# Square roots of layer norms and key lengths as exponential of a logarithm, in a graph transformer kernel

## The chip, the core and the metric

The kernel runs on one core of one Trainium2 chip. A core has five engines that run their own instruction queues in order and wait for each other through semaphores: TensorE (PE in the profile; its weight loads are PEld), VectorE (DVE), ScalarE (ACT), GpSimd (POOL) and SyncE (SP), which only issues DMAs here. The metric is device time in microseconds (us) of one execution.

## The reference

A graph of 3125 nodes with 256 features and 100000 edges passes through two layers, each a graph branch and a mixing branch on the same normalised input, then a feed-forward part.

```python
xn = _layernorm(x, axis=-1)                      # (x - m) / sqrt(v + eps)
x = x + _L0_gnn_ref(xn, ...) + _L0_mix_ref(xn[None], ...)[0]
x = x + _L0_ffn_ref(_layernorm(x, axis=-1)[None], ...)[0]
xn = _layernorm(x, axis=-1)
x = x + _L1_gnn_ref(xn, edge_index, edge_attr_64, ...) + _L1_mix_ref(xn[None], ...)[0]
x = x + _L1_ffn_ref(_layernorm(x, axis=-1)[None], ...)[0]
```

What matters here is where a square root or an exponential is taken:

- `_L0_gnn_ref`: two graph convolutions with 4 heads. Each takes a softmax over the edges of a node (exponentials), and is followed by a batch norm over all nodes, `(x - mean) * rsqrt(var + EPS)`.
- `_L0_mix_ref`: four layers of linear attention. Each has two layer norms, a softmax of the queries and of the keys (exponentials), and a feed-forward part with an exact GELU.
- `_L0_ffn_ref`: 16 experts, of which each token takes two. The two gate values go through a softmax. ReLU inside, a layer norm at the end.
- `_L1_gnn_ref`: one graph convolution with 8 heads and edge features, with the softmax over edges.
- `_L1_mix_ref`: queries and keys are divided by their lengths, `t / maximum(norm(t), 1e-12)`, and enter a second-order expansion.
- `_L1_ffn_ref`: half of the tokens, by the rank of a learned weight, pass through an MLP with the tanh form of GELU.

## The kernel before

**Tiles.** The 3125 nodes are 25 tiles of 125 (`P`), handled in 7 groups of up to four (`k.groups`, six of 4 tiles and one of 1). A layer norm of a group is: `bn_stats` and `bn_aggr` on VectorE for mean and variance (`mv`), a square root with `EPS` added on ScalarE, a reciprocal on VectorE (`rs`, 125 x 4 values), and the scaling of the tiles by it. `ln_stats` (from line 137) does it once for all 25 tiles at the start; `group_stats` (from line 2139) does it for a group in the expert stage and in the last stage.

**Layer 0** runs both branches at once. `SlotOrder.run` writes out by hand the order of the convolution on TensorE, VectorE and ScalarE (`manual_schedule`): for each of 63 steps GpSimd gathers key and value rows (line 707), VectorE multiplies and sums them with the query (lines 1074 and 1077) and takes the maximum (lines 1087 to 1091), ScalarE takes the Exp (line 1101), VectorE sums it (line 1108) and weights the values (line 1114), TensorE adds them up (line 200), and ScalarE copies the sum out (`accT`, line 1133). Four buffers hold the gathered rows. At the marks `m` in that order the planner `Filling` puts pieces of the mixing branch in between. A `Piece` has a weight `w`, a TensorE part `pe`, a part `post` for the other engines, and the pieces that it depends on; the planner issues as much weight at each `m` as its share of the whole comes to, takes the first piece of a window of 8 whose dependencies are done, and issues a piece's `post` only after the TensorE part of the next one. The norm of a group is four pieces (`norm_pieces`, from line 1649): `stats` with the square root (line 1661), `scaled` with the reciprocal (line 1666), the negative mean (line 1667) and the scaling on ScalarE (line 1672), and two that turn the result (lines 1682 and 1689). Line 1763 and line 1821 are the Exps of this branch, line 1999 its GELU.

After each of the two convolutions the batch norm's scale is formed in place (lines 1586 to 1592: aggregate, square root, reciprocal, products).

**The expert stage** (`l0_ffn_routed`) leaves the order to the scheduler. Routing: a norm per group, gate values, the two best of 16 (`top2`, with an Exp at line 2115), and scatters of the tokens to the experts' slots. Then 16 experts, two matrix products each. Then the return, group by group: GpSimd gathers the two results of each token (line 707, tile `g`), VectorE adds them (line 2338), one norm ends the expert layer (lines 2345 and 2348), a second one begins layer 1 (line 152), TensorE turns it and forms the keys and values, which VectorE adds and SP stores (line 2362).

**Layer 1's convolution** (`EdgeOrder`) is again an order by hand, with edge features turned, copied and multiplied (lines 1289, 1295, 1305), added on VectorE (line 1316), and the softmax Exp at line 1324. Pieces of the second mixing branch (`l1_mix_pieces`) fill it. Its planner, `Mixing`, is a little different: a piece has a third part `act`, issued together with `pe`, its `post` comes at the beginning of the next `m`, and a piece with no `post` counts as done at once. Some pieces were already put into the return from the experts (`begin.mixing.ahead`). The branch runs over two halves of the heads, in each over 7 groups of keys and then 7 groups of queries. A group has a head and a body; `spread` puts the pieces of the next group's head behind given places of this group's body, and what has no place behind its end. A head loads the features (`p0`), projects them (`p1`, ending with a Square on ScalarE), and takes the lengths (`p2`): TensorE sums the squares by head (line 3043), ScalarE takes the square root (line 3052, 125 x 16 values), VectorE takes a maximum with 1e-12 and a reciprocal (lines 3095 and 3096 for keys, 3247 and 3248 for queries). For keys the rows follow (line 3114) and `finished` scales them (line 3129); the Squares of the body use the lengths as their scale (line 3168). For queries the lengths are spread over the features by a copy, a transpose and another copy (`widened`, `spread4`, `brought`).

**The last stage** (`l1_ffn`): for each group a norm, a transpose, the row of weights; the row goes to memory and back, VectorE ranks all tokens (line 3606), and the MLP with its GELU (line 3566) runs beside it. The scheduler orders it.

ScalarE evaluates a function from a table that holds a set of functions. The program has an explicit load (`ACT_TABLE_LOAD` in the profile) wherever the next function is not in the set that is loaded; a load stands under the line of the function that it is for. No load stands ahead of a copy, an Identity, a Square or a ReLU in this program.

Of the kernel before, what the change touches and what calls it, by code (L numbers as in the profile page):

```python
# [10 lines left out]
F32 = mybir.dt.float32  # L11
# [8 lines left out]
P = 125  # L20
# [113 lines left out]
    return ap.rearrange("(i p) d -> p i d", p=P)  # L134


def ln_stats(k, pool, src):

    nc = k.nc
    st = pool.tile([P, k.NT, 6], F32, name="ln_st", tag="ln_st")  # L140
    mv = pool.tile([P, k.NT, 2], F32, name="ln_mv", tag="ln_mv")
    rs = pool.tile([P, k.NT], F32, name="ln_rs", tag="ln_rs")
    for i in range(k.NT):
        nc.vector.bn_stats(st[:, i], src[:, i])
        nc.vector.bn_aggr(mv[:, i], st[:, i])
    nc.scalar.activation(rs, mv[:, :, 1], AF.Sqrt, bias=k.eps[:P], scale=1.0)
    nc.vector.reciprocal(rs, rs)
    return mv, rs


# [1303 lines left out]
def l0_gnn_slots(k, dram, order, a, y, pp, pq, cw, filling, tmp):  # L1454
# [45 lines left out]
    with k.tc.manual_schedule(engines=ORDERED):  # L1500
        mix.ahead(30.0)
        prev = None
        for n in (1, 2):
# [81 lines left out]
            prev = hsp  # L1585
            for c in range(2):
                nc.vector.bn_aggr(bmv[:, c], bst[:, c])
            nc.scalar.activation(sc, bmv[:, :, 1], AF.Sqrt, bias=k.eps, scale=1.0)
            nc.vector.reciprocal(sc, sc)
            nc.vector.tensor_tensor(sc, sc, gam, op=ALU.mult)  # L1590
            nc.vector.tensor_tensor(sh, bmv[:, :, 0], sc, op=ALU.mult)
            nc.vector.tensor_tensor(sh, bet, sh, op=ALU.subtract)
# [44 lines left out]
def l0_mix_pieces(k, dram, a, y, wts, one, wp, hp, hp2, pp):  # L1637
# [11 lines left out]
    def norm_pieces(g, deps, weights, free):  # L1649

        g0, ng = k.groups[g]
        o = {}

        def stats():
            st = wp.tile([P, 4, 6], F32, name="ln_st", tag="ln_st")
            o["mv"] = mv = wp.tile([P, 4, 2], F32, name="ln_mv", tag="ln_mv")
            o["rs"] = rs = wp.tile([P, 4], F32, name="ln_rs", tag="ln_rs")
            for j in range(ng):
                nc.vector.bn_stats(st[:, j], y[:, g0 + j])
                nc.vector.bn_aggr(mv[:, j], st[:, j])  # L1660
            nc.scalar.activation(rs[:, :ng], mv[:, :ng, 1], AF.Sqrt, bias=k.eps[:P], scale=1.0)

        def scaled():
            mv, rs = o["mv"], o["rs"]
            nm = wp.tile([P, 4], F32, name="ln_nm", tag="ln_nm")
            nc.vector.reciprocal(rs[:, :ng], rs[:, :ng])
            nc.vector.scalar_tensor_tensor(
                nm[:, :ng], mv[:, :ng, 0], -1.0, rs[:, :ng], op0=ALU.mult, op1=ALU.mult
            )
            o["xh"] = xh = wp.tile([P, 4, D], F32, name="xh", tag="xh")  # L1670
            for j in range(ng):
                nc.scalar.activation(  # L1672
                    xh[:, j], y[:, g0 + j], AF.Identity, bias=nm[:, j : j + 1],
                    scale=rs[:, j : j + 1],
                )

        def turn(c):
            if c == 0:
                o["hT"] = hp2.tile([128, 2, 4 * P], F32, name="hTm", tag="hTm")
            o[c] = ps = ps_tile()  # L1680
            for j in range(ng):
                nc.tensor.transpose(  # L1682
                    ps[:, j * P : j * P + P], o["xh"][:, j, c * 128 : c * 128 + 128],
                    k.ident[:P, :P],
                )

        def bring(c):
            gam, bet = weights()
            nc.scalar.activation(
                o["hT"][:, c, : ng * P], o[c][:, : ng * P], AF.Identity,  # L1690
                bias=bet[:, c : c + 1], scale=gam[:, c : c + 1],
            )

        p1 = Piece(small, None, stats, [*deps, *scales])
        p2 = Piece(small, None, scaled, [p1, *free])
        scales[:] = [p2]
        ts = [Piece(us(ng * P), lambda c=c: turn(c), lambda c=c: bring(c), [p2]) for c in range(2)]
        return [p1, p2, *ts], o
# [440 lines left out]
def group_stats(k, wp, src, ng):  # L2139

    nc = k.nc
    st = wp.tile([P, 4, 6], F32, name="ln_st", tag="ln_st")
    mv = wp.tile([P, 4, 2], F32, name="ln_mv", tag="ln_mv")
    rs = wp.tile([P, 4], F32, name="ln_rs", tag="ln_rs")
    for j in range(ng):
        nc.vector.bn_stats(st[:, j], src[:, j])  # L2146
        nc.vector.bn_aggr(mv[:, j], st[:, j])
    nc.scalar.activation(rs[:, :ng], mv[:, :ng, 1], AF.Sqrt, bias=k.eps[:P], scale=1.0)
    nc.vector.reciprocal(rs[:, :ng], rs[:, :ng])
    return mv, rs  # L2150


# [840 lines left out]
def l1_mix_pieces(k, tabs, a, pl):  # L2993
# [44 lines left out]
        nc.scalar.activation(sq[:, :w_], x[:, :w_], AF.Square)  # L3038

    def by_heads(o, src):  # L3040
        o["p"] = ps = ps_tile()
        for j in range(o["ng"]):
            nc.tensor.matmul(
                ps[:P, j * 4 : j * 4 + 4], src[:, j * P : j * P + P], head0, start=True, stop=True
            )
# [3 lines left out]
        return o[name][:, : o["ng"] * 4]  # L3049

    def root(o):
        nc.scalar.activation(row4(o, "r4"), o["p"][:P, : o["ng"] * 4], AF.Sqrt)

    def widened(o, name):
        n = o["ng"] * 4
# [31 lines left out]
    for c in range(2):  # L3087
        C = {}

        def key_head(g, o, deps, c=c):  # L3090
            ng = o["ng"]

            def lengths():
                r = o["r4"][:, : ng * 4]
                nc.vector.tensor_scalar(r, r, 1e-12, 1.0 / s, op0=ALU.max, op1=ALU.mult)
                nc.vector.reciprocal(r, r)

            def rows(j0, n):
                o["p"] = ps = ps_tile()
                for b in range(n):  # L3100
                    tk = slice((j0 + b) * P, (j0 + b + 1) * P)
                    at = ps[:P, b * D : b * D + D]
                    for ci in range(2):
                        nc.tensor.matmul(
                            at[:, 128:], o["xT"][:, ci, tk],
                            wqkv[:, ci, 2 * D + c * 128 : 2 * D + c * 128 + 128],
                            start=(ci == 0), stop=(ci == 1),
                        )
                    nc.tensor.transpose(at[:, :128], o["x"][:, tk], k.ident)

            def rows_out(j0, n):
                if j0 == 0:
                    o["kv"] = wp.tile([P, 4, 257], F32, name="kvt", tag="kvt")
                nc.scalar.copy(
                    o["kv"][:, j0 : j0 + n, :D],
                    o["p"][:P, : n * D].rearrange("p (b d) -> p b d", d=D),
                )

            def finished():
                kv = o["kv"][:, :ng]  # L3120
                nc.vector.memset(kv[:, :, D:], 1.0)
                v = kv[:, :, 128:D]
                nc.vector.tensor_tensor(
                    v, v, bv[:, c * 128 : c * 128 + 128].unsqueeze(1).to_broadcast([P, ng, 128]),
                    op=ALU.add,
                )
                for j in range(ng):
                    kk = kv[:, j, :128].rearrange("p (h d) -> p h d", d=32)
                    nc.vector.tensor_tensor(
                        kk, kk,  # L3130
                        o["r4"][:, j * 4 : j * 4 + 4].unsqueeze(2).to_broadcast([P, 4, 32]),
                        op=ALU.mult,
                    )

            p0 = Piece(0.0, act=fn(load, o, g, False), deps=deps)
            p1 = Piece(2.3, fn(project, o, 2 + c), deps=[p0], act=fn(squared, o, 2 + c, 1.0))
            p2 = Piece(0.9, lambda: by_heads(o, o["sq"]), lengths, [p1], fn(root, o))
            ps = [
                Piece(0.8 * min(2, ng - j0), fn(rows, j0, min(2, ng - j0)), None, [p1],
                      fn(rows_out, j0, min(2, ng - j0)))  # L3140
                for j0 in range(0, ng, 2)
            ]
            p3 = Piece(0.1, None, finished, [p2, *ps])
            return [p0, p1, p2, *ps, p3]

        def key_body(g, o, head, c=c, C=C):
            ng, g0 = o["ng"], o["g0"]
            p2, p3 = head[2], head[-1]

            def squares():  # L3150
                o["k2"] = wp.tile([P, 4, 128], F32, name="k2", tag="k2")
# [90 lines left out]
        def query_head(g, o, deps, c=c, C=C):  # L3242
            ng, w_ = o["ng"], o["w_"]

            def lengths():
                r = o["r4"][:, : ng * 4]
                nc.vector.tensor_scalar_max(r, r, 1e-12)
                nc.vector.reciprocal(r, r)

            def scaled():  # L3250
                x = o["x"][:, :w_]
                nc.vector.scalar_tensor_tensor(
# [27 lines left out]

            p0 = Piece(0.0, act=fn(load, o, g, True), deps=deps)
            p1 = Piece(2.3, fn(project, o, c), deps=[p0], act=fn(squared, o, c, s))
            p2 = Piece(0.9, lambda: by_heads(o, o["sq"]), lengths, [p1], fn(root, o))
            p2b = Piece(0.1, deps=[p2], act=fn(widened, o, "r4"))
            p3 = Piece(0.6, lambda: spread4(o), scaled, [p2b], fn(brought, o, "far"))
            p4 = Piece(1.2, against, times, [p3, C["made"]], against_out)
            p5 = Piece(0.9, lambda: by_heads(o, o["u"]), inverted, [p4], totals)
            p5b = Piece(0.1, deps=[p5], act=fn(widened, o, "d4"))
            p6 = Piece(0.6, lambda: spread4(o), None, [p5b], fn(brought, o, "inv"))
            return [p0, p1, p2, p2b, p3, p4, p5, p5b, p6]  # L3290

        def query_body(g, o, head, c=c, C=C):
            ng, g0, w_ = o["ng"], o["g0"], o["w_"]
# [68 lines left out]
            for t in range(4):  # L3362
                for h0 in (0, 2):
                    W[t, h0] = Piece(
                        1.2, fn(sums, t, h0), None, [head[4], *(held if h0 == 2 or t else held[:-1])],
                        fn(squared_sums, t, h0),
                    )
                p = Piece(1.2, fn(products, t), None, [W[t, 0], W[t, 2], Y])
# [429 lines left out]
```

## Time and profile before

| | us |
|---|---|
| median of 8 runs | 5318.27 |
| lowest and highest | 5315.63, 5326.0 |
| the profiled execution | 5334.74 |
| its span in the trace | 5332.9 |
| start and order of the nodes | 0 to 291 |
| two convolutions of layer 0 with the batch norm between them | 291 to 2786 |
| end of layer 0 | 2786 to 2884 |
| expert stage: routing, experts, return, pieces ahead | 2884 to 3500 |
| convolution of layer 1 | 3500 to 5095 |
| last stage | 5095 to 5333 |

In the profile, a group row reads: line, engine, operation, output and input tiles, shapes, how often, then busy time and the mean of one in ns, then the idle time of the engine just before them and who ended it. A wait row reads: who waited, for whom, us in total, how often, the longest. A row of windows has each engine's busy time in a stretch and its instructions, then TensorE's granted clock, the DMA share and GB/s. A row of the timeline has its start, its duration, engine, line and operation.

### The profile page before, as it was taken

What the parts mean: (1) busy time and instruction counts of PE and PEld (TensorE: products, weight loads), DVE (VectorE), ACT (ScalarE), POOL (GpSimd) and SP (SyncE); (2) the same over time, 40 slices, a digit from 0 to 9 for tenths busy, and PEclk for the clock granted to TensorE, in tenths of its full rate; (3) what the DMA queues carried; (4) which work ended last, traced back from release to release, by engine and by line L of the source; (5) the groups of instructions that cost most, each with busy time, mean ns of one, the idle gap of its engine ahead of it and who ended that gap; (6) DMA issues with size and microseconds to landing.
All of it is one profiled execution on the core that took longest, in us unless ns stands there. A gap on an engine that the chain in (4) does not pass through costs nothing. (4 is left out here: it accounts for less than half of the span.)

```text
span 5332.9 us, 54974 instructions
## 1 busy us (share of the span) xinstructions
PE 4065.2 (76%) x19016; PEld 2691.2 (50%) x19016; DVE 3909.9 (73%) x5861; ACT 1714.4 (32%) x3630; POOL 3083.8 (58%) x2945
## 2 busy tenths in 40 slices
PE   2557898768876698877875595988888887878778
PEld 1235675556644466555654463345455554544445
DVE  5268888878848888898873223469888888888956
ACT  1023334323343344433343111333333333333221
POOL 2465776657727577666753403257766767776720
PEclk8778999879997799888996797888788888888889
DMA  5166776667737677676765343545665655565610
GB/s 166 51 190 195 211 215 205 185 185 215 214 127 208 186 213 209 204 207 195 224 185 176 120 140 112 172 119 174 178 175 172 184 157 169 168 181 169 181 55 25
DMA packets 374305, 908.90 MB, mean 170 GB/s; under 512 B 94268, under 2 KB 170074, under 8 KB 373892
## 3 DMA queue, kind: packets, MB, share of 16 engines
q0 software_dynamic: 232624, 725.48, 46.9%
q1 hardware_dynamic: 134232, 165.02, 9.6%
q10 hardware_dynamic: 7162, 14.80, 0.7%
q8 instruction: 153, 2.51, 0.2%
q14 instruction: 134, 1.10, 0.1%
HBM read 813.62 MB, written 91.30 MB: 170 GB/s over the span
## 5 line engine op out<-in xcount | busy, mean ns | idle before, releaser
L707 POOL DMA_INDIRECT kv<-kvtab,slots x2499 | 2589.7, 1036 | 1141.6 <-issue 663.2
L1077 DVE TENSOR_REDUCE al<-kv 128x28 f32<-128x1792 f32 (+5 forms) x345 | 719.2, 2085 | 11.9
L200 PEld LDWEIGHTS cps<-ident,kv 128*128 128x128 f32 x4998 | 618.5, 152 | 146.7 <-issue 84.1
L200 PE MATMUL cps<-ident,kv 128*128 128x128 f32 x4998 | 666.9, 290 | 15.7 <-DVE kv L1114 10.4
L1316 DVE TENSOR_TENSOR kv<-kv,e 128x1024 f32<-128x1024 f32 x460 | 489.5, 1113 | 159.7 <-PE e L1305 65.4
L1074 DVE TENSOR_TENSOR kv<-kv,qa 128x1792 f32<-128x1792 f32 (+2 forms) x230 | 478.6, 2081 | 125.3 <-DMA kv<-kvtab,slots 103.1
L1114 DVE TENSOR_TENSOR kv<-kv,qa 128x1792 f32<-128x1792 f32 (+2 forms) x230 | 475.2, 2075 | 0.0
L1991 PE MATMUL mm<-hTm,w 128*128 128x500 f32 (+1 forms) x896 | 377.8, 563 | 30.1 <-DVE xcur L2017 24.1
L2009 PE MATMUL mm<-w,hid 128*125 128x256 f32 x1600 | 384.3, 389 | 11.1 <-ACT hid L1999 10.9
L2009 PEld LDWEIGHTS mm<-w,hid 128*125 128x125 f32 x1600 | 297.7, 194 | 63.1 <-ACT hid L1999 15.9
L1305 PE MATMUL e<-we,eaT 64*128 64x256 f32 x1666 | 288.8, 448 | 35.2 <-ACT eaT L1295 26.0
L1305 PEld LDWEIGHTS e<-we,eaT 64*128 64x128 f32 x1666 | 171.2, 208 | 180.2 <-ACT eaT L1295 60.6
L1991 PEld LDWEIGHTS mm<-hTm,w 128*128 128x128 f32 x896 | 161.2, 201 | 167.0 <-issue 125.8
L1074 DVE TENSOR_TENSOR kv<-kv,q 128x1792 f32<-128x1792 f32 (+2 forms) x115 | 239.3, 2081 | 1.4
L1114 DVE TENSOR_TENSOR kv<-kv,al 128x1792 f32<-128x1792 f32 (+2 forms) x115 | 239.3, 2081 | 0.0
L214 PE MATMUL cps<-ident,accT 128*128 128x128 f32 x378 | 89.1, 323 | 192.2 <-ACT accT L1133 192.0
L1682 PE MATMUL mm<-ident,xh 125*128 125x125 f32 x400 | 102.5, 354 | 169.3 <-ACT xh L1672 158.6
L707 POOL DMA_INDIRECT g<-ys,sloti x50 | 62.7, 1255 | 276.7 <-issue 237.5
L189 PE MATMUL mm<-wqv,hTm 128*125 128x512 f32 x400 | 199.2, 638 | 3.8 <-ACT kT L1763 3.8
L3159 PE MATMUL w<-sel,x 32*125 32x496 f32 x400 | 145.9, 692 | 43.5 <-ACT sq L3168 34.3
L1999 ACT ACTIVATE hid<-mm,b 128x500 f32<-128x500 f32 (+1 forms) x224 | 134.6, 635 | 134.5 <-PE mm L1991 132.9
L214 PEld LDWEIGHTS cps<-ident,accT 128*128 128x128 f32 x378 | 50.9, 160 | 251.0 <-ACT accT L1133 238.3
(421 smaller groups left out, 7247.9 us busy)
## 6 DMA issues: line engine op xcount, KB each, us to landing
kv<-kvtab,slots POOLq DMA_INDIRECT x2499, 3.8
w<-in_L_ffn_w_dram SPq DMA_DIRECT2D x32, 512.0 KB
qd<-qT SPq DMA_DIRECT2D x24, 500.0 KB
kvtab<-st SPq DMA_DIRECT2D x12, 1000.0 KB
qT<-qd SPq DMA_DIRECT2D x24, 500.0 KB
xTg<-xcols SPq DMA_DIRECT2D x24, 500.0 KB
w<-in_L_mix_W_dram SPq DMA_DIRECT2D x8, 1024.0 KB
xs<-zero SPq DMA_DIRECT2D x16, 512.0 KB
```

Of the source, the lines that this page charges most:

```text
L189: nc.tensor.matmul(ps, lhs(c), w(c), start=(c == 0), stop=(bias is None and c == n_chunks - 1))
L200: m = nc.tensor.matmul(ps[:, ch], src[:, ch], k.ident, start=(start and c == 0), stop=stop, is_transpose=True, skip_group_check=True,)
L214: k.nc.tensor.transpose(ps[:, ch], src[:, ch], k.ident)
L707: return k.nc.gpsimd.indirect_dma_start(out=out, out_offset=None, in_=table, in_offset=bass.IndirectOffsetOnAxis(ap=index, axis=0),)
L1074: nc.vector.tensor_tensor(kv[:, :m, :D], kv[:, :m, :D], q.unsqueeze(1).to_broadcast([128, m, D]), op=ALU.mult)
L1077: nc.vector.tensor_reduce(t["al"][:, b0 : b0 + m], self.heads(kv[:, :m, :D]), axis=AX.X, op=ALU.add)
L1114: nc.vector.tensor_tensor(v, v, t["w"][:, b0 : b0 + m].unsqueeze(3).to_broadcast([128, m, H, D // H]), op=ALU.mult)
L1305: self.k.nc.tensor.matmul(e[:, j % 2 * 2 + j // 2], eaT[r, j // 2], self.we[r], start=True, stop=True)
L1316: self.k.nc.vector.tensor_tensor(to, to, e[:, 2 * odd : 2 * odd + n].unsqueeze(2).to_broadcast([128, n, 2, D]), op=ALU.add,)
L1991: nc.tensor.matmul(ps[:, :w_], W["w1"][:, c, j * 128 : j * 128 + 128], o["hT"][:, c, :w_], start=(c == 0), stop=(c == 1),)
L2009: nc.tensor.matmul(ps[:P, :D], s["hid"][:, c, j * P : j * P + P], W["w2"][:, c, :], start=(c == 0), stop=False,)
L3159: nc.tensor.matmul(ps[:P, :496], o["x"][rows, tk], sel[rows], start=True, stop=True, tile_position=((h0 + b) * 32, 0),)
```

## The change

Every square root of a layer norm, of a batch norm and of a key or query length, with the reciprocal behind it, is computed in another way. ScalarE takes the logarithm and then an exponential with the scale -0.5, which gives a rough 1/sqrt (`rough_root`). VectorE refines it with one Newton step in three instructions, `t = (x + eps) * r`, `t = -0.5 * t * r`, `r = (t + 1.5) * r` (`refined_root`). The Sqrt and the reciprocal go. `ln_stats`, `group_stats`, `norm_pieces` and the batch norms do this in the place of the old pair; the step stands where the reciprocal stood.

For the lengths in layer 1, the maximum comes first, with 1e-24 on the square, and reads the sums in the accumulator memory. The piece `p2` becomes two: `p2a` with TensorE's sums and, as its `post`, the maximum and the two ScalarE functions, which so come at the next `m`; and `p2` with the Newton step as its `post`, one `m` later again or more. For keys, `p2` comes after the first of the two pieces of rows. A head has one piece more, so its last piece comes behind the end of the body.

```diff
+def rough_root(k, out, x, bias, scale=1.0):
+    k.nc.scalar.activation(out, x, AF.Ln, bias=bias, scale=scale)
+    k.nc.scalar.activation(out, out, AF.Exp, scale=-0.5)
+
+def refined_root(k, out, t, x, add):
+    nc = k.nc
+    nc.vector.scalar_tensor_tensor(t, x, add, out, op0=ALU.add, op1=ALU.mult)
+    nc.vector.scalar_tensor_tensor(t, t, -0.5, out, op0=ALU.mult, op1=ALU.mult)
+    nc.vector.scalar_tensor_tensor(out, t, 1.5, out, op0=ALU.add, op1=ALU.mult)
...
 def group_stats(k, wp, src, ng):
...
-    nc.scalar.activation(rs[:, :ng], mv[:, :ng, 1], AF.Sqrt, bias=k.eps[:P], scale=1.0)
-    nc.vector.reciprocal(rs[:, :ng], rs[:, :ng])
+    rough_root(k, rs[:, :ng], mv[:, :ng, 1], k.eps[:P])
+    refined_root(k, rs[:, :ng], st[:, :ng, 0], mv[:, :ng, 1], EPS)
...
         def stats():
...
-            nc.scalar.activation(rs[:, :ng], mv[:, :ng, 1], AF.Sqrt, bias=k.eps[:P], scale=1.0)
+            rough_root(k, rs[:, :ng], mv[:, :ng, 1], k.eps[:P])
 
         def scaled():
...
-            nc.vector.reciprocal(rs[:, :ng], rs[:, :ng])
+            refined_root(k, rs[:, :ng], nm[:, :ng], mv[:, :ng, 1], EPS)
...
     def by_heads(o, src):
-        o["p"] = ps = ps_tile()
+        o["p"] = o["by"] = ps = ps_tile()
...
     def root(o):
-        nc.scalar.activation(row4(o, "r4"), o["p"][:P, : o["ng"] * 4], AF.Sqrt)
+        n = o["ng"] * 4
+        o["r2"] = t = wp.tile([P, 2, 16], F32, name="r2", tag="r2")
+        nc.vector.tensor_scalar_max(t[:, 0, :n], o["by"][:P, :n], 1e-24)
+        rough_root(k, row4(o, "r4"), t[:, 0, :n], 0.0)
+
+    def refined(o):
+        n = o["ng"] * 4
+        t = o["r2"]
+        refined_root(k, o["r4"][:, :n], t[:, 1, :n], t[:, 0, :n], 0.0)
...
             def lengths():
+                refined(o)
                 r = o["r4"][:, : ng * 4]
-                nc.vector.tensor_scalar(r, r, 1e-12, 1.0 / s, op0=ALU.max, op1=ALU.mult)
-                nc.vector.reciprocal(r, r)
+                nc.vector.tensor_scalar_mul(r, r, s)
...
-            p2 = Piece(0.9, lambda: by_heads(o, o["sq"]), lengths, [p1], fn(root, o))
+            p2a = Piece(0.8, lambda: by_heads(o, o["sq"]), fn(root, o), [p1])
+            p2 = Piece(0.1, None, lengths, [p2a])
...
-            return [p0, p1, p2, *ps, p3]
+            return [p0, p1, p2a, *ps[:1], p2, *ps[1:], p3]
...
-            p2 = Piece(0.9, lambda: by_heads(o, o["sq"]), lengths, [p1], fn(root, o))
+            p2a = Piece(0.8, lambda: by_heads(o, o["sq"]), fn(root, o), [p1])
+            p2 = Piece(0.1, None, fn(refined, o), [p2a])
...
-            return [p0, p1, p2, p2b, p3, p4, p5, p5b, p6]
+            return [p0, p1, p2a, p2, p2b, p3, p4, p5, p5b, p6]
```

## Prediction

> **What bounds the kernel now.** I read the page's busy shares first, then the windows by stage, the ScalarE groups with shapes apart, VectorE's waits, and the timeline where waits pile up.
>
> ```profile
> span 5332.9 us, 54974 instructions
> PE 4065.2 (76%) x19016; PEld 2691.2 (50%) x19016; DVE 3909.9 (73%) x5861; ACT 1714.4 (32%) x3630; POOL 3083.8 (58%) x2945
> ```
>
> ScalarE, the engine that the change loads, is busy a third of the time: what it gains or loses counts only where somebody waits for it. The windows show who does:
>
> ```profile
> core 0: us, PE busy (x) PEld busy (x) DVE busy (x) ACT busy (x) POOL busy (x), PEclk, DMA share, GB/s
> 291.00:1502.00 1211.00, 940.71 (x4542) 690.30 (x4542) 1002.58 (x1434) 431.42 (x886) 805.97 (x847) 0.87 0.68 201
> 3250.00:3435.00 185.00, 129.99 (x414) 60.55 (x414) 97.47 (x351) 40.97 (x80) 62.50 (x51) 0.76 0.49 159
> 3500.00:5095.00 1595.00, 1294.90 (x6901) 790.93 (x6899) 1381.32 (x1470) 534.12 (x1237) 1109.02 (x911) 0.84 0.58 168
> 5095.00:5333.00 238.00, 195.35 (x702) 123.98 (x702) 152.80 (x281) 62.62 (x103) 34.91 (x24) 0.90 0.11 35
> ```
>
> The convolutions (291 to 2786, twice, and 3500 to 5095) are set by VectorE at 83 to 87%, with GpSimd close behind (each gather is followed by 0.3 us of issue). The return from the experts (3250 to 3435) and the last stage are chains: no engine is full, so latency counts. The chain that ended last covers only 6% of the span and decides nothing.
>
> ```profile
> L1101 ACT ACT_TABLE_LOAD x71 | 91.1, 1283 | 188.6 <-DVE al L1091 128.0 <-DVE top L1149 48.4 <-DVE ln_rs L1666 11.6
> L1999 ACT ACT_TABLE_LOAD x70 | 89.8, 1283 | 15.1 <-PE mm L1991 14.0
> L1661 ACT ACT_TABLE_LOAD x51 | 65.4, 1283 | 64.1 <-DVE ln_mv L1660 63.5
> L1324 ACT ACT_TABLE_LOAD x24 | 30.8, 1283 | 0.4
> L3052 ACT ACT_TABLE_LOAD x23 | 29.5, 1283 | 0.4
> ```
>
> With the smaller rows (9, 5, 4, 3, 3, 2, 1) these are 266 table loads of 1.283 us, 341 us of ScalarE. Who feels them:
>
> ```profile
> DVE den L1108 <- ACT qa L1101: 81.8, 63, 3.8
> DVE r L3095 <- ACT r L3052: 62.9, 8, 23.7
> DVE ln_rs L1666 <- ACT ln_rs L1661: 9.8, 4, 4.5
> DVE ln_rs L2149 <- ACT ln_rs L2148: 5.5, 6, 1.6
> ```
>
> VectorE waits 82 us for layer 0's softmax Exp. Taking each of its 126 Exps from the timeline: 48 have a load that follows a Gelu, and VectorE then stood 65.8 us; 23 have one that follows a square root, 11.5 us in 7 of them; 55 have none, 5.0 us. The square roots themselves are waited for little: from the Sqrt's end to the reciprocal lie 5 us and more in 41 of layer 0's 56.
>
> **What the change does to the loads.** The order of the changed kernel, built but not run, shows a table load ahead of every Ln and another ahead of every Exp that follows it: Ln sits in another set (number 5) than Exp (0), as Sqrt did (3). Of 115 roots, two pairs share a load, so there are 113 + 113 loads at the roots, 48 at the softmax, 70 + 5 at the Gelus: 349 for 266. By stage: 236 for 202 in layer 0; 38 for 7 in the expert stage; 56 for 47 in layer 1's convolution; 19 for 10 at the end. "One table set" does not come about.
>
> The Trainium skill, "ScalarE: Activation LUTs", section "Table sets: the hidden batching unit", says that one set holds both exp and ln, so that ln then exp costs one load; by that rule this order would need 150 loads and ScalarE would gain 149 us. The built order decides against it. The same page, section "What ACT_TABLE_LOAD costs", adds a drain to each switch, 2.66 us in all, which would make the 83 loads cost 221 us; below, the trace shows the next instruction 1.3 us after a load began, so no drain is seen.
>
> **Prices.** The nearest rows:
>
> ```profile
> L1666 DVE RECIPROCAL ln_rs<-ln_rs 125x4 f32<-125x4 f32 x48 | 8.2, 170 | 5.3 <-ACT ln_rs L1661 5.3
> L1667 DVE SCALAR_TENSOR_TENSOR ln_nm<-ln_mv,ln_rs 125x4 f32<-125x4 f32 x48 | 7.9, 166 | 1.6
> ```
>
> ScalarE: 83 loads, 106.5 us; 115 Exps at 0.206 (the small Exp at L2115), 23.7; Ln for Sqrt at the same shape, nothing (small ScalarE instructions of three kinds lie between 0.18 and 0.30, so at most 0.1 either way). Together +130 us. VectorE: three steps for one reciprocal, 3 x 0.166 - 0.170 = 0.33, at 87 norms 28.7; the key lengths gain a maximum (0.20 as L3095), three steps of 0.18 (between 0.166 at 4 columns and 0.21 at 64) and a scaling (0.17) and lose 0.20 and 0.25: 0.46 x 14 = 6.4; query lengths 0.32 x 14 = 4.5. Together +40 us. No DMA and no GpSimd instruction is added; the two loads of a head (on SP) keep their places in the body's order, and only the last pieces of a head fall behind the body's last.
>
> **Stage by stage.** Layer 0 (59 roots). VectorE gets 19 us at 83% busy: 16 on the path. In the timeline, VectorE's idle time that ScalarE ended covers 12.1 of the 69.3 us of Sqrt loads (18%), 4.2 of 17.5 us of Sqrts (24%), and 21.1 of the 38.5 us of the 30 loads from Sqrt to Exp (55%). New: 64 loads' time (82 us) at 18%, 15; Exps 12 at 24%, 3. Gone: 21. Net -3. In the changed order, though, 12 roots have less VectorE work behind them than the 3.06 us of load, Ln, load, Exp, and are short by 25 us together, where the shares give 18. I take +15 (bounds -21, if the gain alone counts, and +75, if 34 loads, 59 Exps and all steps do).
>
> Expert stage. At the routing the scatters run back to back from 2914.7, the first index is ready at 2907.4, so 3 us more is hidden. On the return all 14 roots are without a load today; each becomes 3.06 us for 0.30. The changed order puts 0.7 to 3.5 us of VectorE work over them, short by 21.6 us; VectorE waits 1.9 there today. With 4.6 us of new steps that is 24, of which a quarter hides behind the gathers (21.7 us waited) and the products (27.2): +18 (bounds 0 and +51, counted the same way).
>
> Layer 1's convolution (28 roots, four of them ahead of it). VectorE +11 at 87%: 9.5. Sqrt loads are felt at 5.6 of 29.5 us (19%), the 24 loads ahead of Exp at nothing. New: 33 loads' time, 42 us, at 19%, 8. Gone: 0. **The added wait:** the maximum reads TensorE's sums by head (L3043) on VectorE, with the edge additions (L1316) behind it, and ScalarE's Ln waits for the maximum, with the edge copies (L1295) behind it, for which TensorE's L1305 and then VectorE wait. Before, ScalarE alone waited for those sums, 13.5 us in all. The maximum comes as a `post`, one `m` after the sums, and VectorE is mostly the later engine, so I take nothing, and 28 x 1 us as its bound. +17 (bounds -11, if the later place of the lengths ends VectorE's waits for them in this stage, and +56 with those 28).
>
> Last stage. From 5129 to 5149 ScalarE has hardly a gap:
>
> ```profile
> 5132.06 1.28 ACT L2148 ACT_TABLE_LOAD   x1
> 5133.36 0.30 ACT L2148 ACTIVATE ln_rs<-ln_mv,eps 125x4 f32<-125x4 f32 x1
> 5133.67 1.28 ACT L3566 ACT_TABLE_LOAD   x1
> 5134.97 1.25 ACT L3566 ACTIVATE hid<-mm,b 128x500 f32<-128x500 f32 x2
> ```
>
> Nine more loads and seven Exps are 13 us in the queue that the row of weights, and 100 us of ranking on VectorE behind it, wait for; the order even puts Gelus between Ln and Exp. +10 (bounds 0 and +16).
>
> Sum: 15 + 18 + 17 + 10 = 60 us. The profiled execution takes 5334.7 us, 16 over the median of 5318.3; I add to the median: **5378 us**.
>
> **Rivals.** (1) Faster: the loads that leave the softmax (23 in layer 0, 24 in layer 1) count more than those that join the roots. Place: VectorE at L1108 and, behind it on ScalarE, the copy accT, for which TensorE waits 192 us. Price: 21 us on VectorE and perhaps 1.28 x 23 / 2 = 15 on TensorE, less 8 of steps: 5290. It decides if over nine tenths of the added 130 us lie beside VectorE work. Against it: the expert stage and the end have no such cover. (2) Hidden: at 32% busy ScalarE absorbs it, and the gain at the softmax pays for VectorE's 40 us: 5318. (3) All of it on the path: 130 + 40, 5488; with ScalarE blocked behind VectorE's maximum as well, still that order; half way, 5450.
>
> **Numbers.** Main case 0.70 (5330 to 5440), (1) 0.09, (2) 0.09, (3) 0.12. The range 5312 to 5440 leaves out most of (1) and half of (3). About 0.2% (10 us) is what a measurement can tell: faster 0.09, same 0.09, slower 0.82.
>
> **What would show it.** The new root lines with 113 loads each, 349 in all, ScalarE at some 1845 us, VectorE near 3950; the return from the experts longer by 15 to 25 us, with VectorE waiting for the root's Exp; the last stage longer by 10; L1108's wait shorter by about 10. It is wrong if that return is not longer, or if a convolution changes by more than 25 us, which would be the new order of pieces and not the roots.

## The result, and the profile after

The changed kernel takes 5376.6 us (median of 16 runs) where the kernel before takes 5321.6 (46 runs): a ratio of 1.010, 95% interval 1.009 to 1.011, or 53 us slower (48 to 59). In a later series beside the kernel before it was 1.0112 (1.0088 to 1.0137). The forecast was 5378, 60 us slower.

The profiled execution has a span of 5370.5 us. First the page's busy shares:

```profile
span 5370.5 us, 55267 instructions
PE 4075.8 (76%) x19016; PEld 2683.0 (50%) x19016; DVE 3940.9 (73%) x6105; ACT 1844.3 (34%) x3828; POOL 3089.9 (58%) x2945
```

ScalarE went from 1714.4 to 1844.3 us busy, VectorE from 3909.9 to 3940.9, with 244 more VectorE instructions. No engine is fuller in a way that would explain 53 us by itself: ScalarE has two thirds of its time free.

The windows, laid at the same events as those of before (PE, weight load, DVE, ACT and POOL busy, then granted clock, DMA share and GB/s):

```profile
298.00:1516.00 1218.00, 946.64 (x4542) 691.93 (x4542) 1012.96 (x1492) 459.04 (x932) 806.80 (x847) 0.88 0.68 200
3278.00:3468.00 190.00, 132.85 (x410) 60.91 (x410) 101.24 (x389) 84.89 (x129) 63.03 (x51) 0.77 0.48 154
3528.00:5121.00 1593.00, 1293.41 (x6906) 778.88 (x6904) 1385.31 (x1526) 544.53 (x1269) 1108.14 (x911) 0.86 0.58 168
5121.00:5370.00 249.00, 193.42 (x702) 122.74 (x702) 153.07 (x295) 75.40 (x119) 38.52 (x24) 0.90 0.10 33
```

In the first convolution VectorE has 10 us more to do and the window is 7 us longer. In the return from the experts ScalarE's work doubles (41.0 to 84.9 us) while the window grows by 5. In layer 1's convolution nothing seems to change. The last stage is 11 us longer. What these differences of two single executions are worth is seen further below.

The table loads, from the ScalarE groups with shapes apart (count, busy us, mean ns, then ScalarE's idle time just before them and what ended it):

```profile
L139 ACT ACT_TABLE_LOAD x113 | 145.0, 1283 | 116.5 <-DVE ln_mv L1674 67.2 <-issue 23.1 <-DVE ln_mv L2161 14.6
L140 ACT ACT_TABLE_LOAD x113 | 145.0, 1283 | 4.9 <-issue 2.9
L2013 ACT ACT_TABLE_LOAD x70 | 89.8, 1283 | 7.7 <-PE mm L2005 6.6
L1115 ACT ACT_TABLE_LOAD x48 | 61.6, 1283 | 86.8 <-DVE al L1105 60.8 <-DVE top L1163 25.3
L3585 ACT ACT_TABLE_LOAD x5 | 6.4, 1283 | 0.1
```

349 loads for 266: one for each root's logarithm (L139), one for each root's exponential (L140). "One table set" did not come about. The softmax itself (L1115) did get rid of 23 loads.

VectorE's waits (us in total, times, longest):

```profile
DVE den L1122 <- ACT qa L1115: 62.8, 53, 3.8
DVE ln_st L146 <- ACT ln_rs L140: 53.4, 20, 7.8
DVE ln_nm L146 <- ACT ln_rs L140: 20.1, 10, 6.0
DVE r L3068 <- PE w L3057: 21.4, 5, 9.7
DVE r L146 <- ACT r L140: 19.4, 7, 4.0
```

The wait for the softmax fell by 19 us (81.8 before). VectorE now waits 93 us for the exponentials of the roots, at the first instruction of the Newton step (L146), where it waited 15 us at the reciprocals of the norms and 63 at the key lengths; and it waits another 21 us for TensorE's sums at the new maximum (L3068).

### The profile page after: what moved, and what is told of

The parts are those of the page before. It is cut to its first block, busy times and chain, and to the rows that moved or that the text cites. A ratio compares the mean times of both kernels' runs of the same rounds, so it can differ in the third digit from the quotient of the medians.

```text
span 5370.5 us, 55267 instructions
## 1 busy us (share of the span) xinstructions
PE 4075.8 (76%) x19016; PEld 2683.0 (50%) x19016; DVE 3940.9 (73%) x6105; ACT 1844.3 (34%) x3828; POOL 3089.9 (58%) x2945
## 5 line engine op out<-in xcount | busy, mean ns | idle before, releaser
L1091 DVE TENSOR_REDUCE al<-kv 128x28 f32<-128x1792 f32 (+5 forms) x345 | 719.2, 2085 | 11.9
L1115 ACT ACTIVATE qa<-al 128x56 f32<-128x56 f32 (+7 forms) x126 | 27.3, 216 | 542.5 <-DVE al L1105 396.0
L139 ACT ACT_TABLE_LOAD x113 | 145.0, 1283 | 116.5 <-DVE ln_mv L1674 67.2
```

Source lines behind the costliest of these rows:

```text
L139: k.nc.scalar.activation(out, x, AF.Ln, bias=bias, scale=scale)
L1091: nc.vector.tensor_reduce(t["al"][:, b0 : b0 + m], self.heads(kv[:, :m, :D]), axis=AX.X, op=ALU.add)
```

## The experiments

All ratios are against the kernel before, run on the same chip in the same series; 0.1% is 5.3 us.

### Loads alone, steps alone, order alone

Theory A is the prediction's account; its split of the 60 us by kind is in the expectations. The three edits each do one part of the change.

Loads alone (e1): the reciprocal and the order of pieces stay, and at every root

```diff
-    nc.scalar.activation(rs, mv[:, :, 1], AF.Sqrt, bias=k.eps[:P], scale=1.0)
+    nc.scalar.activation(rs, mv[:, :, 1], AF.Ln, bias=k.eps[:P], scale=1.0)
+    nc.scalar.activation(rs, rs, AF.Exp, scale=0.5)
     nc.vector.reciprocal(rs, rs)
```

> The kernel before with one thing exchanged: each of the 115 square roots is Ln and then Exp of half the logarithm on ScalarE; VectorE's reciprocal and the order of all pieces stay. So it has the 349 table loads and the 115 Exps of the changed kernel and none of its VectorE steps. Theory A (the prediction's: loads and Exps carry about 32 of the 60 us, steps about 28, the order nothing): 5353 us, between 5340 and 5370, ScalarE busy about 1845. Rival B (ScalarE at a third busy hides them, VectorE's steps carry the loss): 5331 at most. Rival C (the new order of the key and query pieces, with its wait of ScalarE for VectorE's maximum, carries half of it): 5336.

Measured: 5349.0 us, ratio 1.0058 (1.0040 to 1.0075): +31 us, between 21 and 40. ScalarE 1845.0 us busy. The trace has 351 table loads, two more than the changed kernel.

Steps alone (e2): square root and reciprocal stay, and behind each reciprocal

```diff
     nc.vector.reciprocal(rs, rs)
+    nc.vector.scalar_tensor_tensor(t, x, EPS, rs, op0=ALU.add, op1=ALU.mult)
+    nc.vector.scalar_tensor_tensor(t, t, -0.5, rs, op0=ALU.mult, op1=ALU.mult)
```

> The kernel before with square root, reciprocal, loads and order of pieces kept, and the Newton step's additional VectorE instructions alone put behind each reciprocal: two per norm and per query length, three per key length, into a scratch tile that nobody reads (they compute nothing that is used). VectorE +40 us busy. Theory A: 5349 us, between 5340 and 5360. Rival B: 5366 or more. Rival C: 5336.

Measured: 5337.5 us, ratio 1.0043 (1.0028 to 1.0057): +23 us, between 15 and 30, for 31 us of VectorE work (3941.2 busy for 3909.9).

Order alone (e3): the changed kernel with

```diff
-    k.nc.scalar.activation(out, x, AF.Ln, bias=bias, scale=scale)
-    k.nc.scalar.activation(out, out, AF.Exp, scale=-0.5)
+    k.nc.scalar.activation(out, x, AF.Sqrt, bias=bias, scale=scale)
...
-    (the three instructions of the Newton step)
+    nc.vector.reciprocal(out, out)
```

> The changed kernel with its order of pieces and with the maximum ahead of the root, for which ScalarE waits, but with a square root on ScalarE and one reciprocal on VectorE in place of logarithm, exponential and Newton step: loads and VectorE work of the kernel before, order and added wait of the changed one. Theory A: 5323 us, between 5313 and 5333. Rival B: the same. Rival C: 5345 or more.

Measured: 5318.3 us, ratio 1.0002 (0.9984 to 1.0020): +1 us, between -9 and +11.

31 + 23 + 1 = 55 us, for 53 and 59 of the whole change. The parts add up: loads and Exps carry about half or somewhat more (the intervals of the two overlap), the VectorE instructions the rest, and the new order with the added wait for the maximum nothing that can be measured. Rivals B (steps alone) and C (order) fall: B had the loads at 10 us at most, C the order at 23 (5331 and 5345 against 5322). Against rival (1) of the prediction, that the loads leaving the softmax count more than those that join the roots, e1 speaks by itself: it has the same shorter wait at the softmax as the changed kernel,

```profile
DVE den L1114 <- ACT qa L1107: 63.0, 53, 3.7
DVE ln_rs L2155 <- ACT ln_rs L140: 62.3, 22, 12.4
```

and is 31 us slower. The second line shows the largest of the new waits: 62 us for the exponentials at the norms by groups, for 5.5 before.

### One set in truth

The profile shows two loads at a root because each function is fetched from a set of its own. Is there a set with both, and what would it bring? The toolchain lets a kernel load a set by name ahead of use:

```diff
+def joint_set(nc):
+    if SET[0] != "joint":
+        nc.scalar.preload_act_table_set("natural_log_exp_and_others")
+    SET[0] = "joint"
...
+    joint_set(k.nc)
     k.nc.scalar.activation(out, x, AF.Ln, bias=bias, scale=scale)
```

with the same call ahead of each softmax Exp, and the mark taken off at each Gelu.

> The changed kernel, instruction for instruction, with the table set that holds both Ln and Exp loaded by name ahead of a root or a softmax where it is not in place, so that the loads at the roots and between root and softmax go: about 150 loads for 349, ScalarE about 1590 us busy. Theory A: the loss by loads (32) goes, and of what the kernel before pays for its own loads of the square root (17 us of waits lie over them) and from square root to softmax (21) most goes too: 5308 us, between 5295 and 5325. Rival B: 5366. Rival C: 5361 less the loads' part of 5 to 15, 5350.

Measured: 5321.0 us, ratio 1.0020 (1.0002 to 1.0038). The kernel was not what the expectation says. The groups show why:

```profile
L143 ACT ACT_TABLE_LOAD x71 | 91.1, 1283 | 9.0 <-DVE ln_mv L170 7.0 <-PEq L3822 0.7
L2034 ACT ACT_TABLE_LOAD x70 | 89.8, 1283 | 7.7 <-PE mm L2025 6.6
L150 ACT ACT_TABLE_LOAD x54 | 69.3, 1283 | 38.3 <-issue 22.4 <-DVE ln_mv L2183 14.7 <-ACT gT L2199 0.4
L151 ACT ACT_TABLE_LOAD x54 | 69.3, 1283 | 3.8 <-issue 2.9
L3609 ACT ACT_TABLE_LOAD x5 | 6.4, 1283 | 0.1
```

Loads by name (L143) serve layer 0; the later stages' roots keep both of theirs (L150 and L151, 54 each). The order was free to place a load that depends on nothing early: two of the named loads stand in the first 10 us of the trace, and none after 2806 us. Even so, some 42 us of the loss is gone (1.0020 for 1.010).

With a dependency from the last Gelu to the named load, and from it to the first function that needs it, the set is in place everywhere:

```diff
+        p = k.nc.scalar.preload_act_table_set("natural_log_exp_and_others")
+        if SET[1] is not None:
+            after(k, p, [SET[1]])
+    ins = k.nc.scalar.activation(*args, **kw)
+    if p is not None:
+        after(k, ins, [p])
```

> The changed kernel with the set that holds both Ln and Exp loaded by name everywhere: some 150 table loads, ScalarE about 1590 us busy. (The last joint kernel had it in layer 0 only: its loads by name for the later stages were placed at the start of the program, and 54 roots there kept both loads.) The named load is free to run before the root's input is there. Theory A (the loads at the roots of the return, of layer 1 and of the last stage cost what the prediction gave them): 5308 us, between 5295 and 5318. Rival (what is left of the loss is VectorE's steps alone, the later loads are hidden): 5321, as the joint set in layer 0 alone.

Measured: 1.0068 (1.0038 to 1.0099), which neither Theory A nor the rival had (the rival was the joint set in layer 0 alone, 1.0020). This series ran on a chip where the kernel before itself takes 5779 us, 8.7% longer (more on it at the end). The changed kernel was not in that series, so the joint kernel was run again beside it, on a chip where the kernel before takes 5311:

> The changed kernel with the joint set everywhere once more, beside the changed kernel itself and one further step, all in one series (the last series was measured at a median of 5779 us for the kernel before, so only its ratios can be used). Theory A: the ratio to before is 0.998 (0.995 to 1.000): the steps' 23 us less what the kernel before pays for its own loads at the roots and between root and softmax. Rival (the last series' ratio holds, the named loads are worth 0.3% and no more): 1.007.

Measured: 5301.1 us, ratio 0.9985 (0.9970 to 1.0001).

> The changed kernel, unchanged, beside the two others: 1.010 of before. If this series is measured under the conditions of the last one, the three places' sum there (0.24, 0.40 and 0.49%) makes it 1.0113.

Measured: 5373.5 us, ratio 1.0112 (1.0088 to 1.0137). With the same VectorE work (3941.9 us busy) and the same 115 Exps the joint kernel takes 72 us less by the medians (67 by the ratios), with 205 table loads fewer and with the ties that hold the others in place. From its page and its groups:

```profile
PE 4054.6 (77%) x19016; PEld 2676.7 (51%) x19016; DVE 3941.9 (74%) x6105; ACT 1583.3 (30%) x3623; POOL 3080.1 (58%) x2945
L144 ACT ACT_TABLE_LOAD x72 | 92.4, 1283 | 2.1 <-PEq L3819 0.7
L155 ACT ACT_TABLE_LOAD x72 | 92.4, 1283 | 7.7 <-PE mm L2026 6.6
```

144 loads, half of them at Gelus (L155). One more thing is to be read in the idle column: ahead of its loads at L139 the changed kernel's ScalarE stood 116.5 us, mostly for VectorE's means and variances. There a load put in just ahead of the function that needs it stood behind the wait for that function's input; the loads by name had 2.1 us ahead of them. So part of the 72 us may be that a load no longer stands behind a wait; the two were not told apart.

### Without the steps

What the joint kernel still has beyond the kernel before is the steps, the extra Exps and the order of pieces. Exp of minus half the logarithm is already the reciprocal root, so the kernel before can be given this and lose its reciprocals too:

```diff
-            nc.scalar.activation(rs[:, :ng], mv[:, :ng, 1], AF.Sqrt, bias=k.eps[:P], scale=1.0)
+            joint(k, rs[:, :ng], mv[:, :ng, 1], AF.Ln, bias=k.eps[:P], scale=1.0)
+            joint(k, rs[:, :ng], rs[:, :ng], AF.Exp, scale=-0.5)
...
-            nc.vector.reciprocal(rs[:, :ng], rs[:, :ng])
...
-                nc.vector.tensor_scalar(r, r, 1e-12, 1.0 / s, op0=ALU.max, op1=ALU.mult)
-                nc.vector.reciprocal(r, r)
+                nc.vector.tensor_scalar(r, r, 1e12, s, op0=ALU.min, op1=ALU.mult)
```

> The kernel before with its order of pieces, logarithm and exponential in the joint set loaded by name, and nothing on VectorE: Exp of minus half the logarithm is the reciprocal root, without Newton step and without reciprocal (the accuracy is that of ScalarE's tables). About 150 loads, VectorE 115 reciprocals (20 us busy) below the kernel before. Theory A: 0.9925 of before (0.989 to 0.996), which is the joint kernel less 23 us of steps and some 12 of reciprocals and maxima. Rival: 1.000 to 1.003, if the joint kernel is at 1.007.

Measured: 5276.8 us, ratio 0.9929 (0.9912 to 0.9946): 38 us faster than the kernel before and about 97 faster than the changed one. VectorE is at 3893.4 us, 16.5 below the kernel before, ScalarE at 1578.7 with 144 loads. Its last stage is still 7 us longer than before (see the table), so there may be more to be had. This kernel differs from the joint one in three things at once (steps, reciprocals, order of pieces); of these the order alone was worth nothing measurable.

### The places

The change was also made in one place at a time. The first three ran on the chip with 5779 us for the kernel before; their microseconds below are their ratios times 5315, which takes it that the ratios hold on the other chips.

> The kernel before with the changed roots in layer 0 alone (the norms of its pieces, the one ahead of them, the batch norm: 59 of 115). Theory A, the prediction's terms by place: +15, 5330 us. Rival D, which takes the places from the two profiled executions (the layer's end 29 us later): +29, 5344.

Measured: 1.0024 (1.0000 to 1.0047), +13 us of 5315, between 0 and 25, which fits Theory A and leaves rival D out.

> The kernel before with the changed roots in the norms by groups alone (7 at the routing, 14 at the return from the experts, 7 in the last stage: 28 of 115). Theory A: +18 at the return and +10 at the end, 5343 us. Rival D: +7 and +12, 5334.

Measured: 1.0040 (1.0017 to 1.0063), +21 us, between 9 and 33: both 28 and 19 lie inside.

> The kernel before with the changed roots in the lengths of keys and queries alone (28 of 115), with their new order of pieces and the maximum ahead of the root. Theory A: +17, 5332 us. Rival D: -7 to 0, 5308 to 5315.

Measured: 1.0049 (1.0026 to 1.0072), +26 us, between 14 and 38: rival D falls. And once more on a chip with 5314 us for the kernel before:

> The kernel before with the changed roots in the key and query lengths alone, measured once more, since the series of the places ran at 5779 us for the kernel before. Theory A (the term of the prediction): 1.0032 of before, +17 us. Rival (the ratio of that series holds): 1.0049, +26. Rival D (the profiled executions of the changed kernel show layer 1's convolution at 1563 and 1571 us for 1564): 1.000, between -5 and +5 us.

Measured: 5343.8 us, ratio 1.0059 (1.0044 to 1.0075): +31 us (23 to 40). The term of the prediction, 17, and rival D both lie outside; the ratio of the earlier series lies inside. The two single executions had shown nothing there at all.

Why the two traces misled is seen when the stages of all profiled executions on the faster chips stand side by side (us between the same events in each; worked out from the starts of the instructions: the last score sum of layer 0, the last instruction of the experts' first product, layer 1's first and last score sum, the first row of ranks):

| execution | to layer 0's end | return and pieces ahead | layer 1's convolution | from there to the ranks |
|---|---|---|---|---|
| before | 2766 | 274 | 1564 | 103 |
| order alone (e3) | 2770 | 261 | 1564 | 101 |
| lengths alone (e12) | 2768 | 280 | 1568 | 100 |
| loads alone (e1) | 2772 | 278 | 1564 | 111 |
| steps alone (e2) | 2772 | 272 | 1552 | 100 |
| changed | 2794 | 273 | 1563 | 115 |
| changed (e11) | 2780 | 281 | 1571 | 115 |
| joint in layer 0 (e4) | 2746 | 273 | 1563 | 115 |
| joint (e9) | 2737 | 264 | 1553 | 121 |
| no steps (e10) | 2726 | 264 | 1554 | 110 |

Layer 0 is the steadiest: three executions that leave it as it was lie within 4 us. Layer 1's convolution is 1552 us with 10 us more VectorE work in it (e2) and 1564 without; differences of 10 us there say nothing. A profiled execution also need not be a typical one: that of the steps alone took 5320.6 us, 17 below its median. The kernel before was profiled at 5334.7 us, 16 above its median at the time, and the return and the convolution behind it are where that execution was long. Against it the changed kernel seems to lose nothing from the experts to layer 1's end; against e3, which has the same order of pieces, it loses 12 and 27 us there.

In the return itself the waits show the mechanism. VectorE's waits between the experts and layer 1's convolution, order alone:

```profile
DVE r L3065 <- PE w L3054: 28.6, 3, 10.8
DVE acc L2349 <- DMA g<-ys,sloti: 22.1, 12, 8.6
DVE kvt L3142 <- ACT kvt L3133: 21.2, 3, 10.7
```

the same stretch of the changed kernel:

```profile
DVE ln_st L146 <- ACT ln_rs L140: 24.0, 9, 7.8
DVE kvt L3145 <- ACT kvt L3136: 21.9, 3, 11.1
DVE acc L2352 <- DMA g<-ys,sloti: 20.0, 12, 8.3
DVE st L2376 <- PE mm L203: 17.7, 9, 6.8
DVE r L3068 <- PE w L3057: 16.2, 2, 9.7
DVE r L146 <- ACT r L140: 6.8, 3, 2.5
```

and of the kernel before:

```profile
DVE r L3095 <- ACT r L3052: 54.8, 4, 23.7
DVE st L2362 <- PE mm L189: 27.2, 11, 12.5
DVE kv L1316 <- PE e L1305: 24.3, 1, 24.3
DVE acc L2338 <- DMA g<-ys,sloti: 21.7, 12, 8.7
DVE kvt L3123 <- ACT kvt L3114: 2.4, 3, 1.0
```

The wait for the roots by groups is new and it is the one forecast (24.0 us at L146). But the kernel before stood 54.8 us at L3095, four times, for the root of the lengths of the pieces ahead. With the new order of pieces and the maximum ahead of the root that wait is split up: order alone has 28.6 at the maximum (L3065) and 21.2 at the scaling of the rows (L3142, 2.4 before), 50 us for 57. The changed kernel has 16.2 and 21.9 there and 6.8 at its roots of the lengths, 45 us, so between these single executions a part of what it lost at the norms came back at the lengths. That the new order shortens the kernel is not shown: alone it was worth +1 us, between -9 and +11.

In the last stage the queue of ScalarE is what the prediction said. The changed kernel:

```profile
5172.38 1.28 ACT L140 ACT_TABLE_LOAD   x1
5173.67 0.20 ACT L140 ACTIVATE ln_rs<-ln_rs 125x4 f32<-125x4 f32 x1
5173.89 1.28 ACT L3585 ACT_TABLE_LOAD   x1
5175.19 1.25 ACT L3585 ACTIVATE hid<-mm,b 128x500 f32<-128x500 f32 x2
5176.45 1.28 ACT L139 ACT_TABLE_LOAD   x1
```

Exp, Gelu and Ln each fetch a set in turn, and the ranking starts 115 us after the convolution, for 103. The loads do this and not the steps: 111 with the loads alone, 100 with the steps alone. The joint kernel does no better there (121), for another cause. Its named load was tied to the last Gelu ahead of it, and with that tie eight Gelus came to stand in one row ahead of the load, ScalarE idle for 1 us before each until TensorE had the next (the last two are shown):

```profile
5095.43 0.68 ACT L155 ACTIVATE hid<-mm,b 128x500 f32<-128x500 f32 x1 [1.00 <-PE mm L3602]
5097.10 0.68 ACT L155 ACTIVATE hid<-mm,b 128x500 f32<-128x500 f32 x1 [1.00 <-PE mm L3602]
5097.80 1.28 ACT L144 ACT_TABLE_LOAD   x1
5099.18 0.48 ACT L147 ACTIVATE ln_rs<-ln_mv,eps 125x4 f32<-125x4 f32 x2
```

VectorE waits 14.7 us for the first of the Exps behind them:

```profile
DVE ln_st L167 <- ACT ln_rs L147: 30.6, 8, 14.7
```

The kernel without steps has the same ties and the same row of eight Gelus (its 110 in the table). Few loads and a bad place in the queue cost as much in this stage as many loads.

## Why the prediction was right, and where it was not

- **The loads.** "349 for 266", 113 at each of the two new lines, ScalarE at "some 1845 us": 349, 113 and 113, 1844.3. This came from the built order, not from the diff.
- **The sum.** 60 us forecast; 53 and 59 measured. By kind: loads and Exps 32 forecast, 31 measured; VectorE's steps 28 and 23; the added wait for the maximum 0 and 1.
- **VectorE's work.** +40 us forecast, +31 measured. The prices were near: the new steps took 0.154 to 0.178 us each, and the durations of all that came sum to 64.5 us, of all that went to 26.7, so +38. But VectorE's busy time counts a stretch once in which two of its instructions overlap (in the changed kernel, durations of 4210.3 us make 3940.9 busy), and this overlap grew by 9 us.
- **The softmax's wait.** "Shorter by about 10": shorter by 19. That it did not pay is what rival (1) had wrong: e1 has all of that gain.
- **Layer 0, +15.** e6 has +13 (0 to 25); the two traces of the changed kernel reach the layer's end 13 to 26 us later than the three executions that left it alone (2768 on average). Right within what can be told. The 15 was a choice and not a sum: its own parts give 16 - 3 = 13, or 20 with the 25 us that the order leaves uncovered.
- **Return +18 and last stage +10, 28 together.** e7 has +21 (9 to 33). The last stage is 12 us longer in both traces. In the trace of e7 it is 10 us longer too (112 for 102 in that of e6), so that term stands. The return failed the test that the prediction set for it: "longer by 15 to 25" was 5 by the windows, and -1 and +7 by the events of the table. Of this the step that failed is "VectorE waits 1.9 there today": it counted the wait at the norms and not the 54.8 us at L3095 in the same stretch, which the new order of pieces, costed at nothing, splits up. The prediction had the row (62.9 us in all) and did not set it beside the return. How much of the miss comes from this, and how much from a long profiled execution of the kernel before, stays open.
- **Layer 1's lengths, +17.** Measured alone, +31 (23 to 40) and +26 on the chip with 5779 us. The mis-sized step is "33 loads' time, 42 us, at 19%, 8", or its place: it prices all 28 roots by the share felt in the convolution. The profile of the lengths alone shows the convolution 4 us longer than with the order alone and the return with the pieces ahead of it 19 us longer. The kernel with the lengths alone has only 11 table loads more than the kernel before (277 for 266), so their number alone does not explain it: 56 stand at these roots where 23 did, and the 24 that went from the softmax had cost nothing by the prediction's reading. That would put most of it on the few roots ahead of the convolution. The traces of the slower chip point the same way (that return takes 316 us with the lengths alone, 291 with layer 0 alone; the convolution 1688 and 1693). But it rests on one execution each, in stretches that vary by 10 us on the one chip and by 36 on the other, and stays open.

So the total was met partly by luck: the lengths were 14 us too low, the groups and layer 0 were 9 too high (both within their intervals), and the places measured alone (13, 21 and 31, each within about 8 to 12) sum to 65 us, some 6 to 12 more than the whole change. The kinds were priced well, the places less so. In the rivals, the 5450 of "half way" in (3) does not follow from its 170 us, half of which gives 5403; no run came near either.

The prediction also weighed a section of the Trainium skill, "ScalarE: Activation LUTs", "Table sets: the hidden batching unit", which has one set for exp and ln. Both are true: the set exists, and the joint kernel shows it at work with 144 loads; but in this program Ln and Exp each got a set of their own (113 loads at each of the two lines) until the kernel named the joint one. The estimate made with it (ScalarE gains 149 us by 116 fewer loads) leaves out the 115 Exps, some 24 us; measured were 122 fewer loads (157 us) and 131 us gained.

## What to carry to other kernels

Before trusting that two functions share a table set, count the loads in the built order, and if the set exists but is not taken, load it by name and tie that load into the order: here the same arithmetic was 1.1% slower than before without this, and with it no slower. Then look at where the tied load put its neighbours. A refinement in small VectorE instructions cost most of its time here, where VectorE is the fullest engine of the long stages (23 of 31 us, between 15 and 30), so ask first whether the tables' accuracy needs it. Do not read a stage's gain or loss from two single executions: repeat the profile, or change that stage alone, before a difference of 10 us in a stage of 1564 is given a cause.

## What was not expected

- **A chip that is 8.7% slower for the same kernel.** One series ran at a median of 5779 us for the kernel before (34 runs, 5750 to 5810). The lengths alone were profiled there and on another chip, so the two traces are of one kernel. On the slower chip TensorE and ScalarE have much idle time that ends with nothing the trace shows, 444 and 341 us summed as "issue", for 45 and 31 on the other, and ScalarE another 560 us put down to "remote", which the other trace does not have; the first convolution of layer 0 takes 1338 us for 1185 between its first and last score sum. VectorE's score sums are 719.2 us busy in both, but TensorE is 4232.2 us busy for 4077.3, at a granted clock of 0.827 for 0.853. What holds the engines up there was not found. The named sets were worth less on it: 1.0068 for the joint kernel, for 0.9985.
- **One price for a load over the whole kernel, and none by place.** Going from 266 to 351 loads (e1) lost 31 us, with 115 Exps in it: 0.36 us for a load. Going from 349 to 144, by name, won 72: 0.35. So where ScalarE is a third busy a load of 1.283 us cost a little over a quarter of itself, on the average of all stages. By place it does not hold: layer 0 alone has 34 loads more than before and cost 13 us, the groups 45 and 21, the lengths 11 and 31, with the steps in all three. The number of loads alone does not give the price of a place.
- **After a load, the next function starts 1.29 us after the load began** (5172.38 to 5173.67 above) where it waits for nothing else, in the changed kernel as in the kernel before: the load's own 1.283 us, and nothing on top.
